# A new written order for the first steps of a two-layer graph network, and looks queued behind the gates

## The chip, the cores and the metric

The kernel runs on one core of a Trainium2 chip. The metric is device microseconds from start to end. The core has five engines with instruction queues of their own: PE (TensorE, matrix products), DVE (VectorE), ACT (ScalarE), POOL (GpSimd) and SP (SyncE, which here only issues transfers). Each executes its queue in order; they wait for each other by semaphores.

## The reference

Sixteen batches of 1024 nodes with 128 features, and one 1024x1024 adjacency matrix of zeros and ones for each. Layer 0 is a gated graph network (four steps, GRU cells), layer 1 a convolution (four steps) with a normalisation over all batches. Both have a norm over the features in front and a residual around.

```python
# layer 0
h = jnp.maximum(_layernorm(x, axis=-1), 0.0)
x = x + gated(h)                # four steps i, for each batch:
#   hw = h @ weight[i];  m = einsum('bjn,bjd->bnd', adj, hw)
#   gx = m @ w_ih[i].T + b_ih[i];  gh = h @ w_hh[i].T + b_hh[i]
#   r = sigmoid(xr + hr); z = sigmoid(xz + hz); n = tanh(xn + r * hn)
#   h = (1 - z) * n + z * h
# layer 1
h = jnp.maximum(_layernorm(x, axis=-1), 0.0)
x = x + conv(h)                 # four steps: adj @ (h @ W[i]) + b[i], relu, norm over (b, n)
```

## The kernel before

`exact_path` does the work; a second path runs only if an entry of the adjacency is found that a 16-bit mantissa can't hold. That finding is the **look** (L568): for each of the eight row blocks of a batch (128 rows, 128x1024 values, 512 KB) DVE takes the maximum of the low 16-bit halves into a column of `low`. All columns are reduced once at the end.

The gated layer runs two batches beside each other, as streams `sa` and `sb` (class `Stream`, L647). Each step of a stream has these parts:

- `split_step` (L688): the features are turned by eight PE transposes into node-major form (at step 0 the normed input `y` has that form already), and split into a high part (ACT) and a low part (DVE), both fp32r, `ghw`.
- `agg_step` (L702): the aggregation, 32 matmuls of 128x512 into the two PSUM banks `pm`, four for each row block: high part to both banks, then low part to both. The weight of the step is folded into the GRU's input matrix, so the aggregation takes the bare features. ACT then copies `pm` to `m`.
- `gate_step` (L713), for each of two halves of 512 nodes: six fp32 products on PE into four PSUM banks `g_r`, `g_hn`, `g_xn`, `g_z`, of which there is one each; sigmoid on ACT (frees `g_r`), two operations on DVE (free `g_hn` and `g_xn`), tanh and sigmoid on ACT (frees `g_z`), three operations on DVE (L738 to L740).

`half_step(one, two)` (L783) puts the gates of one stream and the aggregation of the other after each other. In it `two.ahead()` (L747) prepares the stream's next batch: it loads `x` at step 1, takes its norm at step 2 (`prepare`: statistics on DVE, square root on ACT, scale on DVE, eight ACT blocks `y_in`), and turns it at step 3. `one.look_on()` (L767) starts the transposes of the rows for layer 1 (POOL casts a block to bf16, a transposing DMA follows) and looks at three row blocks a step. From step 1 on only SP and POOL follow the written order; a scheduler lays out PE, DVE and ACT, and `tc.issue_after(ins)` forbids it to put an instruction ahead of `ins` on the same engine. Looks stand behind `self.seen`, the last DVE operation of that stream's own step-0 gates; the norm stands behind the gates' last ACT operation only, so its DVE part stands free.

The first steps (L803 to L847) are written out by hand for all engines. Batch 0 and 1 have no bf16 or fp32r copy in memory, so their rows arrive as raw fp32: four blocks in a `stage` buffer, four in `h` tiles, and POOL or ACT rounds them to fp32r row tiles. The order there: 52 idle transposes on PE; x of batch 0 and 1; rows of batch 0; weights of step 0; norm of x0 whole; aggregation; all eight looks; then the rows of batch 1 into the buffers the looks have left; small vectors, turning of `y`, weights of step 0 (`turn_layer`, L463: seven transposes, a product `w_gT @ w_ihT`, and four DVE copies out of the two PSUM banks `tmp`); norm of x1; gates of batch 0; aggregation and looks of batch 1; weights of steps 1 to 3. Of the `x` tiles there are four, one of them holding `w_g`.

Of the kernel before, what the change touches and what calls it, by code (L numbers as in the profile page):

```python
# [16 lines left out]
P = 128  # L17
# [324 lines left out]
def exact_path(  # L342
# [68 lines left out]
    low = const.tile([P, B * NB], F32, tag="low", name="low")  # L411
# [50 lines left out]

    def turn_layer(prep, w_g, i):  # L463

        pt = tmp(f"pt_whh{i}")
        for g in range(3):
            nc.tensor.transpose(pt[:, g * P : (g + 1) * P], wns["hh", i][:, g, :], ident)
        nc.vector.tensor_copy(w_hhT[:, i, :], pt[:, : 3 * P])
        pt = tmp(f"pt_wih{i}")
        for g in range(3):  # L470
            nc.tensor.transpose(pt[:, g * P : (g + 1) * P], wns["ih", i][:, g, :], ident)

        w_ihT = prep.tile([P, 3 * C], F32, tag="w_ihT", name=f"w_ihT{i}", bufs=1)
        nc.vector.tensor_copy(w_ihT, pt[:, : 3 * P])
        pg = tmp(f"pt_g{i}")
        nc.tensor.transpose(pg[:, :P], w_g[:, i, :], ident)
        w_gT = prep.tile([P, P], F32, tag="w_gT", name=f"w_gT{i}", bufs=1)
        nc.vector.tensor_copy(w_gT, pg[:, :P])
        pw = tmp(f"pt_wm{i}")
        nc.tensor.matmul(pw[:, : 3 * P], w_gT, w_ihT, start=True, stop=True)  # L480
        nc.vector.tensor_copy(w_mT[:, i, :], pw[:, : 3 * P])
# [45 lines left out]
    with ExitStack() as st:  # L527
# [15 lines left out]
        def load_rows_first(b, stage):  # L543

            fs = []
            for j in range(NB):
                if j < 4:
                    f = stage[:, 2 * j : 2 * j + 2, :].rearrange("p a n -> p (a n)")
                else:
                    f = work.tile([P, N], F32, tag="h", name=f"first{b}_{j}", bufs=7)  # L550
                nc.sync.dma_start(f, adj[b][j * P : (j + 1) * P, :])
                fs.append(f)
            return fs
# [14 lines left out]
        def look(b, row, j):  # L568

            lows = row.bitcast(U16).rearrange("p (n t) -> p n t", t=2)[:, :, 0]  # L570
            k = b * NB + j
            nc.vector.tensor_reduce(low[:, k : k + 1], lows, axis=AX.X, op=ALU.max)  # L572
# [7 lines left out]
        def norm(xt, y, name):  # L580

            norm_apply(xt, y, name, norm_stats(xt, name))

        def norm_stats(xt, name):
            stats = small.tile([P, NB, 6], F32, tag="ln_st", name=f"st_{name}")
            mv = small.tile([P, NB, 2], F32, tag="ln_mv", name=f"mv_{name}")
            for k in range(NB):
                nc.vector.bn_stats(stats[:, k, :], xt[:, k, :])
                nc.vector.bn_aggr(mv[:, k, :], stats[:, k, :])
            return mv  # L590

        def norm_apply(xt, y, name, mv, split=None):
            rs = small.tile([P, NB], F32, tag="ln_rs", name=f"rs_{name}")
            nc.scalar.activation(rs, mv[:, :, 1], AF.Sqrt, bias=eps_t)
            nc.vector.reciprocal(rs, rs)
            ms = small.tile([P, NB], F32, tag="ln_ms", name=f"ms_{name}")
            nc.vector.scalar_tensor_tensor(ms, mv[:, :, 0], -1.0, rs, ALU.mult, ALU.mult)
            for k in range(NB):
                nc.scalar.activation(
                    y[:, k * P : (k + 1) * P], xt[:, k, :], AF.Relu, bias=ms[:, k : k + 1], scale=rs[:, k : k + 1]  # L600
                )
                if split and k % BH == BH - 1:
                    split(k // BH)
# [13 lines left out]
        def tail_norm(b, xt, hT):  # L617

            for hf in range(NH):
                pt = tmp(f"pt_x{b}_{hf}")  # L620
                for q in range(BH):
                    k = hf * BH + q
                    nc.tensor.transpose(pt[:, q * P : (q + 1) * P], hT[:, k * P : (k + 1) * P], ident)
                for q in range(BH):
                    k = hf * BH + q
                    nc.vector.scalar_tensor_tensor(
                        xt[:, k, :],
                        pt[:, q * P : (q + 1) * P],
                        maskT[:, b * NB + k : b * NB + k + 1],
                        xt[:, k, :],  # L630
                        ALU.mult,
                        ALU.add,
                    )
            mv = norm_stats(xt, f"mid{b}")
            if b + 1 < B:
                y = work.tile([P, N], F32, tag="h", name=f"y_mid{b}", bufs=7)
            else:
                y = xt.rearrange("p k c -> p (k c)")
            nc.gpsimd.dma_start(xmid_d[b].rearrange("(k p) c -> p k c", p=P), xt)

            def rest():
                norm_apply(xt, y, f"mid{b}", mv)
                nc.gpsimd.dma_start(ymid_d[b], y)

            return rest

        class Stream:  # L647
# [5 lines left out]
            def open(self, xt):  # L653

                self.xt = xt
                self.y = work.tile([P, N], F32, tag=f"y{self.tag}", name=f"y_in{self.b}", bufs=1)
                self.mv = norm_stats(xt, f"in{self.b}")

            def open_split(self):

                self.hw = hw_tiles(self.b, f"ghw{self.b}_0")
                norm_apply(self.xt, self.y, f"in{self.b}", self.mv, self.split_first)

            def open_rows(self, fs, on_scalar):
                self.rows, self.looks = [], NB
                for j, f in enumerate(fs):
                    t = gru_row(self.b, j)
                    if j in on_scalar:
                        nc.scalar.copy(t, f)
                    else:  # L670
                        nc.gpsimd.tensor_copy(t, f)
                    self.rows.append(t)
# [15 lines left out]
            def split_step(self):  # L688
                nm = f"{self.b}_{self.i}"
                self.hw = hw_tiles(self.b, f"ghw{nm}")  # L690
                for g in range(NH):
# [3 lines left out]
                    self.split_first(g)  # L695

            def split_first(self, g):
                hi, lo, y = (t[:, g * HALF : (g + 1) * HALF] for t in (*self.hw, self.y))
                nc.scalar.copy(hi, y)  # L699
                nc.vector.tensor_sub(lo, y, hi.bitcast(F32))  # L700

            def agg_step(self, g):  # L702
                if g == 0:
                    self.pm = [acc(f"m{hf}", f"pm{self.b}_{self.i}_{hf}") for hf in range(NH)]
                aggregate(self.pm, self.hw, self.rows, g)
                if g == NH - 1:
# [6 lines left out]
            def gate_step(self, hf):  # L713
# [20 lines left out]
                nc.vector.tensor_add(r, pxn, r)  # L734
                nc.scalar.activation(r, r, AF.Tanh, bias=b_in(i))  # L735
# [4 lines left out]
                last = nc.vector.tensor_add(ho, ho, r)  # L740
                if i == 0:
                    self.seen = last
# [4 lines left out]
            def ahead(self):  # L747
# [5 lines left out]
                if self.i == 2:  # L753
                    with tc.issue_after(self.last_act.ins):
# [12 lines left out]
            def look_on(self):  # L767
# [10 lines left out]
                with tc.issue_after(self.seen.ins):  # L778
# [4 lines left out]
        def half_step(one, two):  # L783
# [4 lines left out]
            two.gate_step(1)  # L788
            if one.i == 0:
                one.split_step()  # L790
            one.agg_step(0)
            if one.rest:
                with tc.issue_after(two.last_act.ins):
# [3 lines left out]
            one.look_on()  # L797
# [5 lines left out]
        with tc.tile_pool(name="prep", bufs=1) as prep, tc.manual_schedule(engines=every):  # L803
# [3 lines left out]
            for k in range(52):  # L807
                nc.tensor.transpose(pt[:, k % 4 * P : (k % 4 + 1) * P], ident, ident)
            x0, x1 = load_x(0, nc.sync), load_x(1, nc.sync)
            small_in = load_small(prep)  # L810
            stage = keep.tile([P, NB, N], BF16, tag="adjT", name="stage", bufs=1).bitcast(F32)
            rows0 = load_rows_first(0, stage)
            h0 = work.tile([P, N], F32, tag="h", name="h_in0", bufs=7)
            load_layer(0)
            w_g = flat("w_g")[:, :L, :]
            nc.sync.dma_start(w_g, g_weight.rearrange("l c d -> c l d"))

            sa.open(x0)
            sa.open_split()
            sb.open(x1)  # L820
            sa.open_rows(rows0, (4, 5, 6, 7))
            sa.agg_step(0)
            for j, f in enumerate(rows0):
                look(0, f, j)
            rows1 = load_rows_first(1, stage)
            for i in range(1, L):
                load_layer(i)
            h1 = work.tile([P, N], F32, tag="h", name="h_in1", bufs=7)
            sa.agg_step(1)
            turn_small(*small_in)  # L830
            turn(sa.y, "in0", h0)
            turn_layer(prep, w_g, 0)
            sa.hT = h0
            sb.open_split()
            turn(sb.y, "in1", h1)
            sb.hT = h1
            sb.open_rows(rows1, ())
            nc.gpsimd.dma_start(w_c, c_w.rearrange("l c d -> c l d"))
            sa.gate_step(0)
            sa.gate_step(1)  # L840
            sb.agg_step(0)
            sb.agg_step(1)
            for j, f in enumerate(rows1):
                look(1, f, j)
            for i in range(1, L):
                turn_layer(prep, w_g, i)
            sa.ahead()  # L847
        with tc.manual_schedule(engines={mybir.EngineType.Pool, mybir.EngineType.SP}):
            for s in range(1, B // 2 * L):
# [260 lines left out]
```

## Time and profile before

| what | value |
|---|---|
| median of 3 runs | 1871.44 us (1869.63 to 1871.64) |
| profiled execution | 1870.41 us |
| its span, first to last instruction | 1868.6 us |
| PE busy | 1827.9 us, 98% |
| DVE / ACT / POOL busy | 65% / 56% / 15% |
| granted PE clock | 0.991 of full, mean |

The gated layer takes the first 1250 us or so, the convolution the rest. A matmul's time in the profile is its latency; how densely PE works shows in the distance between starts. A row of the timeline has its start, its time, the engine and line, what is written from what, how many instructions it merges, and in brackets the idle time before it and what ended that.

### The profile page before, as it was taken

The numbers are of one execution on the slowest core, as the hardware profiler recorded it, in microseconds if no ns is written. First come the engines' busy times: TensorE is split into PE (matmuls) and PEld (weight loads), VectorE is DVE, ScalarE is ACT, GpSimd is POOL, SyncE is SP. The second block draws the span as 40 slices with busy tenths as digits, with TensorE's granted clock in tenths as the row PEclk, the third lists the DMA queues.
The fourth block names the chain that finished last, engine by engine and source line by source line (L and its number), as shares of the span: only waits on it lengthen the run. The fifth ranks groups of instructions, "written<-read, shape, count | busy, mean of one in ns | idle before, by whom it ended". The sixth has DMA issues, their size and how long they took to land.

```text
span 1868.6 us, 21940 instructions
## 1 busy us (share of the span) xinstructions
PE 1827.9 (98%) x7328; PEld 1257.9 (67%) x7328; DVE 1215.2 (65%) x2242; ACT 1041.8 (56%) x1569; POOL 287.8 (15%) x369
## 2 busy tenths in 40 slices
PE   7999999999999999999999999999999999999995
PEld 5666656565656666666656665667778888888884
DVE  5746864775684595586476577576666666666664
ACT  4353553554454455455356453357777768768764
POOL 3121230221042032023023113000000000000021
PEclk8999999999999999999999999999999999999998
DMA  7487476485376567557548546339876676666768
GB/s 260 118 231 259 156 204 191 149 239 179 124 225 198 186 166 228 192 162 204 217 139 224 169 149 145 128 126 334 301 245 228 212 250 214 237 235 216 251 211 260
DMA packets 267824, 381.21 MB, mean 204 GB/s; under 512 B 149716, under 2 KB 171896, under 8 KB 263864
## 3 DMA queue, kind: packets, MB, share of 16 engines
q1 hardware_dynamic: 250032, 246.21, 43.7%
q0 software_dynamic: 17456, 133.45, 20.3%
q8 instruction: 59, 0.97, 0.2%
q14 instruction: 61, 0.50, 0.1%
q10 hardware_dynamic: 216, 0.08, 0.0%
HBM read 287.39 MB, written 117.44 MB: 217 GB/s over the span
## 4 chain that ended last, share of the span: by engine, by line
PE 42%; issue 5%; DVE 3%; DMA 3%; POOL 1%; ACT 1%; SPq 0%; DVEq 0%; POOLq 0%; ACTq 0%
PE pc_m L518 12%; PE pc_g_z L518 6%; PE pc_g_r L518 6%; PE pm L518 4%; PE hw_c L493 4%; PE g_z L722 2%; PE g_r L722 2%; DMA adjT<-half 2%; DVE low L572 1%; PE g_xn L722 1%; PE pt_o L1054 1%; PE g_hn L722 1%; PE pw_g_hn L935 1%; PE pw_g_xn L935 1%; PE pc_g_r L503 1%
## 5 line engine op out<-in xcount | busy, mean ns | idle before, releaser
L518 PE MATMUL pm<-row,ghw 128*128 128x512 f32 x2048 | 506.7, 404 | 2.1 <-ACT ghw L699 2.1
L518 PEld LDWEIGHTS pm<-row,ghw 128*128 128x128 f32 x2048 | 385.0, 189 | 107.4 <-issue 31.9
L518 PE MATMUL pc_m<-wide,chw 128*128 128x512 f32 x1024 | 246.1, 396 | 0.0
L518 PEld LDWEIGHTS pc_m<-wide,chw 128*128 128x128 f32 x1024 | 190.6, 188 | 42.2 <-issue 4.3
L735 ACT ACTIVATE r<-r,vecs 128x512 f32<-128x512 f32 x128 | 92.3, 721 | 213.3 <-DVE r L734 213.2
L518 PE MATMUL pc_g_r<-wide,chw 128*128 128x512 f32 x464 | 187.2, 404 | 0.3 <-ACT chw L495 0.3
L518 PE MATMUL pc_g_z<-wide,chw 128*128 128x512 f32 x464 | 181.3, 391 | 0.0
L577 POOL CAST half<-row 128x1024 bf16<-128x1024 f32 x128 | 141.5, 1122 | 247.0 <-DMA adjT<-half 166.4
L880 DVE CAST wide<-packed 128x1024 fp32r<-128x1024 bf16 x160 | 110.3, 693 | 74.6 <-PE pc_m L518 56.3
L880 DVE CAST wide<-block 128x1024 fp32r<-128x1024 bf16 x160 | 110.3, 692 | 73.3 <-PE pc_g_z L518 35.1
L736 ACT ACTIVATE z<-g_z,brz 128x512 f32<-128x512 f32 x128 | 87.3, 682 | 121.2 <-PE g_z L722 121.2
L496 DVE TENSOR_TENSOR ghw<-hw_g,ghw 128x512 fp32r<-128x512 f32 x96 | 61.7, 683 | 118.7 <-ACT ghw L495 118.7
L722 PE MATMUL g_xn<-m,w_mT 128*128 128x512 f32 x256 | 131.9, 597 | 4.9 <-DVE r L734 4.9
L878 ACT CAST wide<-block 128x1024 fp32r<-128x1024 bf16 x96 | 100.6, 1048 | 60.9 <-PE pc_m L518 34.4
L878 ACT CAST wide<-packed 128x1024 fp32r<-128x1024 bf16 x96 | 100.7, 1049 | 56.5 <-PE pc_g_z L518 27.4
L722 PE MATMUL g_r<-m,w_mT 128*128 128x512 f32 x256 | 131.6, 596 | 0.0
L572 DVE TENSOR_REDUCE low<-row 128x1 f32<-128x1024 uint16 x112 | 130.8, 1201 | 0.0
L722 PE MATMUL g_z<-m,w_mT 128*128 128x512 f32 x256 | 130.8, 593 | 0.0
L732 ACT ACTIVATE r<-g_r,brz 128x512 f32<-128x512 f32 x128 | 87.7, 685 | 61.0 <-PE g_r L722 59.8
L738 DVE TENSOR_TENSOR h<-h,r 128x512 f32<-128x512 f32 x96 | 68.9, 718 | 78.7 <-ACT r L735 78.7
L733 DVE SCALAR_TENSOR_TENSOR r<-g_hn,vecs,r 128x512 f32<-128x512 f32 x128 | 95.0, 742 | 35.8 <-PE g_hn L722 18.6
L710 ACT COPY m<-pm 128x512 f32<-128x512 f32 x128 | 68.0, 582 | 87.5 <-PE pm L518 87.5
(142 smaller groups left out, 2774.0 us busy)
## 6 DMA issues: line engine op xcount, KB each, us to landing
packed<-adjT_d SPq DMA_DIRECT2D x256, 256.0 KB, 5.7
block<-adjT_d SPq DMA_DIRECT2D x256, 256.0 KB, 5.3
raw<-in_adj_dram POOLq DMA_DIRECT2D x112, 512.0 KB, 11.7
row<-raw SPq DMA_DIRECT2D x112, 512.0 KB, 6.2
adjT_d<-adjT POOLq DMA_DIRECT2D x16, 2048.0 KB, 7.2
xmid_d<-x POOLq DMA_DIRECT2D x16, 512.0 KB, 4.2
y<-ymid_d POOLq DMA_DIRECT2D x16, 512.0 KB, 5.4
xo<-xmid_d POOLq DMA_DIRECT2D x32, 256.0 KB, 6.1
```

What stands on the lines that cost most here:

```text
L493: nc.tensor.matmul(pt[:, q * P : (q + 1) * P], src, w, start=True, stop=True)
L518: nc.tensor.matmul(pm[hf], hw[s][:, j * P : (j + 1) * P], rows[j][:, hf * HALF : (hf + 1) * HALF], start=(j == 0 and s == 0), stop=(j == N ...
L572: nc.vector.tensor_reduce(low[:, k : k + 1], lows, axis=AX.X, op=ALU.max)
L577: nc.gpsimd.tensor_copy(t, row.bitcast(F32))
L722: nc.tensor.matmul(po, wT[:, i, g * C : (g + 1) * C], rhs, start=start, stop=stop)
L732: nc.scalar.activation(r, pr, AF.Sigmoid, bias=brz[:, 3 * i : 3 * i + 1])
L733: nc.vector.scalar_tensor_tensor(r, phn, b_hn(i), r, ALU.add, ALU.mult)
L735: nc.scalar.activation(r, r, AF.Tanh, bias=b_in(i))
L736: self.last_act = nc.scalar.activation(z, pz, AF.Sigmoid, bias=brz[:, 3 * i + 1 : 3 * i + 2])
L738: nc.vector.tensor_sub(ho, hin, r)
L878: nc.scalar.copy(r, t)
L880: nc.vector.tensor_copy(r, t)
```

## The change

It does five things. The norm of x0 is taken in two halves, x0 arrives in two halves through two queues (SP and ACT). The turning of `y`, the small vectors and the weights of step 0 stand between the row blocks 3 and 6 of the first aggregation. The rows of batch 1 are loaded into unused tiles first (the first four blocks as eight halves), ahead of the looks; a look at a half row has a column of its own, so `low` grows by two batches of columns and is cleared. The norm of x1 stands beside the first gates, and the weights of steps 1 to 3 each between two half steps. And in the rest of the gated layer the looks are put behind the last DVE operation of the other stream's gates just before them, the norm behind the last ACT and the last DVE operation of the gates.

```diff
     def turn_layer(prep, w_g, i):
...
         nc.vector.tensor_copy(w_gT, pg[:, :P])
+        turned[i] = w_gT, w_ihT
+
+    def join_layer(i):
+        w_gT, w_ihT = turned[i]
         pw = tmp(f"pt_wm{i}")
         nc.tensor.matmul(pw[:, : 3 * P], w_gT, w_ihT, start=True, stop=True)
         nc.vector.tensor_copy(w_mT[:, i, :], pw[:, : 3 * P])
...
+        def behind(*inss):
+
+            es = ExitStack()
+            for ins in () if written[0] else inss:
+                es.enter_context(tc.issue_after(ins.ins))
+            return es
...
+                if between:
+                    between()
                 nc.scalar.activation(r, r, AF.Tanh, bias=b_in(i))
...
                 if self.i == 2:
-                    with tc.issue_after(self.last_act.ins):
+                    with behind(self.last_act, self.last_dve):
                         self.prepare(self.b + 2, self.next_x)
...
-            def look_on(self):
+            def look_on(self, two):
...
-                with tc.issue_after(self.seen.ins):
+                with behind(two.last_dve):
                     while self.looks < min(3 * self.i, NB):
...
-        def half_step(one, two):
+        def half_step(one, two, gated=None, halfway=None):
...
             two.gate_step(1)
+            if gated:
+                gated()
...
             one.agg_step(0)
+            if halfway:
+                halfway()
...
-            for k in range(52):
+            for k in range(50):
...
-            x0, x1 = load_x(0, nc.sync), load_x(1, nc.sync)
+            x0 = flat("x0")
+            for k0, eng in ((0, nc.sync), (BH, nc.scalar)):
+                x0_d = x[0].rearrange("(k p) c -> p k c", p=P)[:, k0 : k0 + BH, :]
+                eng.dma_start(x0[:, k0 : k0 + BH, :], x0_d)
...
+            first_rows(0, range(4), quarters)
             load_layer(0)
...
+            nc.sync.dma_start(w_g[:, 0, :], w_d[:, 0, :])
+            first_rows(0, range(4, NB), late)
+            x1 = load_x(1, nc.sync)
...
+            first_rows(1, range(4), halves)
...
+            sa.sums(range(4))
+            norm_root(sa.norm, 0, BH)
+            sa.sums(range(4, 5))
+            norm_scale(sa.norm, 0, BH)
+            sa.sums(range(5, NB))
+            sa.normed(range(2))
+            norm_root(sa.norm, BH, NB)
+            norm_scale(sa.norm, BH, NB)
+            sa.normed(range(2, 4))
+            sa.split_high(0)
+            for j in range(4):
+                sa.rows[j] = first_round(0, j, raw0[j], nc.gpsimd)
+            first_look(0, 0, raw0[0])
+            sa.split_low(0)
+            sa.agg_rows(range(4))
+            sa.normed(range(4, NB))
+            sa.split_high(1)
+            first_look(0, 1, raw0[1])
+            sa.split_low(1)
+            for j, eng in ((4, nc.scalar), (5, nc.gpsimd)):
+                sa.rows[j] = first_round(0, j, raw0[j], eng)
+
+            turn_small(*small_in)
+            turn(sa.y, "in0", h0)
+            sa.hT = h0
+            first_look(0, 2, raw0[2])
+            turn_layer(prep, w_g, 0)
+            first_look(0, 3, raw0[3])
+            first_rows(1, range(4, NB), quarters)
+            sa.agg_rows(range(4, 6))
+            join_layer(0)
+            for j, eng in ((6, nc.scalar), (7, nc.gpsimd)):
+                sa.rows[j] = first_round(0, j, raw0[j], eng)
+            sa.agg_rows(range(6, NB))
+
+            sb.sums(range(NB))
+            norm_root(sb.norm, 0, NB)
+            norm_scale(sb.norm, 0, NB)
+            for j in range(NB):
+                sb.rows[j] = first_round(1, j, raw1[j], nc.gpsimd)
+
+            def beside(hf):
+                sb.normed(range(hf * BH, (hf + 1) * BH))
+                first_look(0, 4 + hf, raw0[4 + hf])
+
+            for hf in range(NH):
+                sa.gate_step(hf, lambda: beside(hf))
+                sb.split_high(hf)
+                sb.split_low(hf)
+            for j in (6, 7):
+                first_look(0, j, raw0[j])
+            for j in range(4):
+                first_look(1, j, raw1[j])
...
+            sb.agg_rows(range(4))
             turn(sb.y, "in1", h1)
             sb.hT = h1
+            sb.agg_rows(range(4, NB))
             sa.ahead()
+
+            def looks():
+                for j in range(4, NB):
+                    first_look(1, j, raw1[j])
+
+            half_step(sa, sb, looks, lambda: turn_layer(prep, w_g, 1))
+            join_layer(1)
+            half_step(sb, sa, None, lambda: turn_layer(prep, w_g, 2))
+            join_layer(2)
+            turn_layer(prep, w_g, 3)
+            join_layer(3)
...
-            for s in range(1, B // 2 * L):
+            written[0] = False
+            for s in range(2, B // 2 * L):
                 half_step(sa, sb)
                 half_step(sb, sa)
```

`first_rows` loads row blocks, `first_round` rounds them on ACT or POOL, `first_look` looks at each part; `norm_sums`, `norm_root`, `norm_scale` and `norm_blocks` are the four parts of the norm, and `sums`, `normed`, `split_high` and `split_low` call them and the two parts of the split for a stream.

As built, the scheduler's order of the rest of the gated layer changes with it. Before, all eight looks of a batch stand in one row on DVE, partly between the operations of the gates. After, they stand in threes behind the gates; in the half step in which a stream reaches step 2, DVE has the statistics of the next batch's norm and three looks behind the gates, then the norm's scale, then the low parts of the split, and ACT has the eight `y_in` blocks ahead of the high parts (in the next half step between the two high parts). PE has four matmuls of the aggregation pulled between the two halves of the gates there, and nine in the next half step.

## The prediction

> **What bounds the kernel now.** First the page: the busy times and the forty slices.
>
> ```profile
> PE 1827.9 (98%) x7328; PEld 1257.9 (67%) x7328; DVE 1215.2 (65%) x2242; ACT 1041.8 (56%) x1569; POOL 287.8 (15%) x369
> ...
> PE   7999999999999999999999999999999999999995
> ```
>
> PE sets the end. Only time in which PE waits, or runs at half clock, can be won. I took dense distances between PE starts from the timeline (0.227 us for an aggregation matmul, 0.43 for a gate's, 0.109 for a turn) and summed what exceeds them: 47.7 us in the whole span. Of it 17.8 lie between the first aggregation (11.88) and the end of the second aggregation of batch 1 (98.95), 10.4 in the looks' stages between 200 and 1200, 9 at the last normalisation, which the change leaves alone.
>
> The first steps, in stretches of 10 us (after each engine's busy time comes the granted clock):
>
> ```profile
> 10.00:20.00 10.00, 8.12 (x28) 6.27 (x29) 6.46 (x21) 7.87 (x13) 2.91 (x3) 0.83 0.91 330
> 20.00:30.00 10.00, 4.71 (x21) 3.43 (x20) 7.54 (x11) 2.44 (x5) 4.95 (x5) 0.68 0.98 347
> 30.00:40.00 10.00, 7.30 (x18) 3.15 (x17) 2.60 (x7) 6.68 (x13) 5.10 (x6) 0.67 0.92 270
> 40.00:50.00 10.00, 10.00 (x25) 4.68 (x24) 7.64 (x24) 2.81 (x6) 0.00 (x0) 0.96 0.00 0
> ```
>
> Then the timeline of DVE and PE there:
>
> ```profile
> 22.25 4.59 DVE L572 TENSOR_REDUCE low<-first 128x1 f32<-128x1024 uint16 x4
> 26.76 0.18 DVE L448 COPY vecs<-pt_v 128x36 f32<-128x36 f32 x1
> ...
> 11.88 9.39 PE L518 MATMUL pm<-row,ghw 128*128 128x512 f32 x32 [2.09 <-ACT ghw L699]
> ...
> 27.00 1.97 PE L613 MATMUL pt_in<-ident,y_in 128*128 128x128 f32 x8 [5.29 <-DVE vecs L448]
> ...
> 33.79 1.63 PE L613 MATMUL pt_in<-ident,y_in 128*128 128x128 f32 x4 [1.48 <-ACT y_in L599]
> ...
> 37.41 1.92 PE L722 MATMUL g_r<-h_in,w_hhT 128*128 128x512 f32 x2
> ```
>
> A 0.18 us copy stands behind eight looks and holds PE for 5.3 us; the clock falls, and the first gates start at 37.41 although their aggregation ended at 21.27.
>
> Then a look stage, timeline at 238 us:
>
> ```profile
> 238.30 1.20 DVE L572 TENSOR_REDUCE low<-row 128x1 f32<-128x1024 uint16 x1
> 239.42 0.68 DVE L734 TENSOR_TENSOR r<-g_xn,r 128x512 f32<-128x512 f32 x1
> ...
> 240.15 1.13 PE L722 MATMUL g_xn<-m,w_mT 128*128 128x512 f32 x2 [0.60 <-DVE r L734]
> ```
>
> Looks between the gates' DVE operations free the one bank `g_xn` late. Such half steps take up to 1.4 us more than an undisturbed one; per pair of batches 1.8, 1.1, 2.2, 1.3, 1.5, 1.2 and 1.3 us, together 10.4.
>
> **The first steps, worked out.** x0's first half should land at 4.4, an estimate: the whole let DVE start at 4.99, less about half of the 1.29 us that 512 KB take here. Four blocks of statistics at 0.395: 6.0. Root 0.30, one more block, reciprocal 0.20, scale 0.54: 7.15. Two `y_in` blocks 0.85: 8.05. The second root waits for statistics until 8.4 and ends at 8.7, two blocks 9.5, high part 0.62: PE starts at 10.15, not 11.88. Row 0 is looked at before the low part is made (9.3 to 11.15), which costs PE 0.6. Rows 0 to 3 end at 14.4. x1 now loads behind all rows of batch 0, so these rows land no later (17.2 for the last, at the 1.29 us a block of before).
>
> From 14.4 to 17.1 PE does small vectors, turning and seven transposes, 1.84 us of work; each waits for a `tmp` bank that DVE (0.18 to 0.56 a copy, one look of 1.14 between) or ACT (0.59) empties: 0.9 lost. Rows 4 and 5: 18.95. Product: 19.6. Rows 6 and 7: 21.4. The first gates start at 21.4, 16.0 earlier, at full clock, and end at 31.7. Beside them: statistics of x1 20.2 to 23.4, table load 1.28, sigmoid free at 25.75; the second half's `g_r` needs it at 26.6, so no wait. Batch 1's blocks land until 28.8 (9.5 MB at the same pace) and POOL has rounded them by 30; block 4 is wanted at 36.2. The norm's second low part comes at 36.8 and costs 0.15. Batch 1's aggregation ends at 40.0 (before: 56.7).
>
> Gates of batch 1: 40.9 to 51.2. DVE owes ten looks from 36.8 (two whole, eight halves at about 0.6, estimated from 1.14 a whole) until 43.9; `g_hn` is wanted at 47.7, so hidden.
>
> Then the new wait. PE's order is four row blocks, the transposes of step 1's weights, four blocks. DVE ends the gates at 53.9 and has four looks (4 x 1.145) ahead of the copy `w_hhT`: 58.5, copied at 59.1. `pt_g` is the third user of two banks and has stood since 55.5: 3.6 lost, and behind it the rest of the aggregation. Half clock after it: before, 2.1 us of idle at 9.8 was followed by one cold stretch of 3.4 us in which 16 matmuls took 0.427 each; I put 1.3 of the possible 1.7. The joins and steps 2 and 3 lose 1.5 more, their copies being only 0.5 apart from the products.
>
> Sum of losses 0.6 + 0.9 + 0.15 + 3.6 + 1.3 + 1.5 = 8.05, so (11.88 + 17.8) - (10.15 + 8.05) = **11.5 us won**. Bounds: x0's half could land with the whole (0.6 less) and each new gap could bring its own cold stretch (2.8 less), or neither the 1.3 nor half of the small waits come (2.5 more): 8 to 14.
>
> POOL is let go later: `x` of batch 3 waits for the tile of `w_g`, whose last turn moves from 71 to about 88, and behind it in POOL's queue stand the raw copies and casts, behind these SP's transposes. They end by 165; batch 2's rows are wanted at 173. Hidden by 10 us; without that cover each late us costs one.
>
> Costed at nothing: the clearing of `low` (DVE waits for x0 until 4.4), two idle transposes fewer, the half x0 issued by ACT ahead of its table load (0.65 more; the load ended at 4.47 and the root is wanted at 6.0; without that cover 0.1), 16 more columns in the last reduction, and SP's loads of the later weights behind tiles that the looks free at 44 (about 48; wanted at 54.8, each us beyond would lengthen the new wait).
>
> The Trainium skill, "TensorE: Matmul & The Clock Gate", Part 4, says that transposes don't count as PE work for the clock. This trace shows otherwise: its idle transposes go from 0.213 to 0.109 us apart at 6.8 and PE starts warm. By the page the transposes put between the rows would let the clock fall once more, 1.7 us at its half rate; by the row nothing.
>
> **The looks, worked out.** Gone: 10.4. New: in the half step in which a stream reaches step 2, everything is queued behind the gates. Let T be the gates' end on PE. DVE ends the gates at T+h; statistics 2.2, three looks 3.45, reciprocal and scale 0.45; ACT then has eight `y_in` blocks 3.18, the two high parts 1.05, a table load 1.30, and only then the sigmoid 0.69 that frees `g_r`: T+h+12.4. PE wants it at T + 7.27 (aggregation) + 0.87 + 5.16 (half the gates) + 0.91 (four pulled matmuls) = T+14.2. Wait: h - 1.8. In the next half step nine matmuls are pulled and one high part comes first: h - 2.6. The rows for the prices:
>
> ```profile
> 265.93 3.19 ACT L599 ACTIVATE y_in<-x,ms_in,rs_in 128x128 f32<-128x128 f32 x8 [0.47 <-DVE ms_in L597]
> ...
> 271.05 1.28 ACT L732 ACT_TABLE_LOAD   x1
> ...
> 277.11 1.41 DVE L739 TENSOR_TENSOR h<-h,z 128x512 f32<-128x512 f32 x1
> ```
>
> Undisturbed, h is 2.4. Beside POOL's casts it was 2.3 to 5.0 (the third line: 1.41, not 0.69), and casts fall in both half steps. I take 3.2 for both, nearer to the half steps without a second table load: 1.4 + 0.6 = 2.0 a pair, in the six pairs that have both norm and looks: 12.0. Net **1.8 lost**. Bounds: h = 2.4 gives 0.6 x 6 = 3.6, net 6.8 won; h = 4.9 and 4.2 give (3.1 + 1.6) x 6 = 28, net 18 lost.
>
> Total 11.5 - 1.8 = 9.7 from the profiled 1870.4: 1860.7. The median of the runs lies 1.0 above that execution: **1862**. Own range 1856 to 1867.
>
> **Rivals.** (1) *Both gains come*: POOL's casts miss the gates, h is 2.4: 11.5 + 6.8 = 18 won, 1853. For it: in three of seven pairs h was 2.3 to 2.4 in the second of these half steps. Against: POOL's casts fill 4 to 6 us around the first. (2) *The norm held up by the looks becomes the bound, slower*: one mechanism, the chain statistics, looks, scale, `y_in`, sigmoid, in twelve half steps. At 4.7 a pair 18 are lost against 11.5 won: 1878. It decides from 3.65 a pair ((11.5 + 10.4) / 6). For it: POOL casts in every such pair. Against: it needs nearly the highest h of the trace in each. (3) *The first steps give back more*: the stall before step 1's weights grows as DVE is later than I have it, each gap goes cold, and 11.5 shrinks to 3: 1870. For it: DVE has no slack between 20 and 59. Against: PE's waits up to 51 have 0.8 to 4 us of room.
>
> **How the numbers follow.** Forecast 0.53, (1) 0.17, (2) 0.12, (3) 0.18. No change means within 0.2% (3.7 us), 1867.7 to 1875.2; a measurement of this kernel tells no less. Faster: 0.51 + 0.17 + 0.03 = 0.71; same: 0.02 + 0.03 + 0.14 = 0.19; slower 0.10. The range reaches from (1) to short of (2): 1853 to 1874.
>
> **What would show it.** Right: first aggregation at about 10.2; first gates at about 21.4 and end of batch 1's first aggregation near 40; PE waiting 3 to 4 us at `pt_g` behind `w_hhT` near 55; no PE wait for L734's bank `g_xn` among looks; in pairs 1 to 6 a PE wait of 1 to 2 us at `g_r` for ACT's sigmoid once a pair, none in the last pair. Wrong: gates starting after 26, a PE wait at the aggregation for rows or for `ghw` in the first steps, waits at `g_r` over 3 us in each pair, or batch 2's rows late.

## The result, and the profile after

The changed kernel takes 1866.06 us (median of 12 runs, 1864.58 to 1869.47) against 1871.64 for the kernel before beside it (12 runs, 1869.32 to 1872.88). The medians lie 5.6 us apart; the ratio is 0.9973, 95% interval 0.9964 to 0.9982: between 3.4 and 6.7 us won. Predicted were 1862 and a gain of 9.7; 1866.06 lies inside the forecast's own range and at its upper end.

The profiled execution has a span of 1863.3 us (before 1868.6). The page's rows that answer to those of before:

```profile
PE 1825.8 (98%) x7326; PEld 1255.0 (67%) x7326; DVE 1226.6 (66%) x2249; ACT 1032.4 (55%) x1562; POOL 290.3 (16%) x375
...
PE   9999999999999999999999999999999999999995
```

The 7 in the first slice has become a 9. The first steps in the same stretches of 10 us (PE, PEld, DVE, ACT, POOL busy, then the granted clock):

```profile
10.00:20.00 10.00, 8.88 (x35) 6.19 (x36) 6.02 (x11) 5.50 (x10) 3.96 (x4) 0.83 1.03 360
20.00:30.00 10.00, 10.00 (x32) 5.72 (x31) 6.54 (x24) 4.88 (x9) 6.69 (x10) 1.00 1.05 391
30.00:40.00 10.00, 9.74 (x37) 5.84 (x35) 9.21 (x12) 6.79 (x13) 4.28 (x5) 1.00 0.34 96
40.00:50.00 10.00, 9.72 (x35) 6.04 (x36) 9.78 (x15) 2.84 (x7) 0.00 (x0) 1.00 0.35 98
...
60.00:70.00 10.00, 7.42 (x28) 5.69 (x29) 3.83 (x7) 1.71 (x4) 0.00 (x0) 0.83 0.00 0
```

From 20 to 40 PE is now busy 10.00 and 9.74 of each 10 us, where it had been busy 4.71 and 7.30. The lost time now sits in the first and the last of these rows. The timelines of PE and DVE show both places:

```profile
10.41 0.70 PE L525 MATMUL pm<-row,ghw 128*128 128x512 f32 x2 [1.47 <-ACT ghw L733]
11.42 5.06 PE L525 MATMUL pm<-row,ghw 128*128 128x512 f32 x14 [0.31 <-DVE ghw L737]
...
24.00 1.02 PE L762 MATMUL g_r<-h_in,w_hhT 128*128 128x512 f32 x2
...
40.28 3.48 PE L525 MATMUL pm<-row,ghw 128*128 128x512 f32 x14 [0.47 <-DVE ghw L737]
...
62.37 0.33 PE L479 MATMUL pt_g<-ident,w_g 128*128 128x128 f32 x1 [3.10 <-DVE w_hhT L471]
62.45 5.50 PE L525 MATMUL pm<-row,ghw 128*128 128x512 f32 x16
...
57.26 4.59 DVE L589 TENSOR_REDUCE low<-stage 128x1 f32<-128x1024 uint16 x4
61.77 0.55 DVE L471 COPY w_hhT<-pt_whh 128x384 f32<-128x384 f32 x1
```

The first gates start at 24.00 (before 37.41, predicted 21.4). The wait at `pt_g` behind four looks is there as predicted (3.10), and the 16 matmuls behind it take 5.34 us, from the first one's start to the start of what follows, in place of 3.63. What was not predicted is that the 14 matmuls at 11.42 take 5.06 us. The same two places by granted clock (the same columns as above):

```profile
10.00:13.40 3.40, 2.67 (x8) 1.89 (x9) 3.19 (x4) 2.44 (x6) 1.87 (x2) 0.81 0.97 321
13.40:16.80 3.40, 3.40 (x11) 2.36 (x10) 0.10 (x1) 1.04 (x1) 1.04 (x1) 0.68 1.02 414
62.00:65.40 3.40, 3.03 (x10) 2.41 (x11) 1.03 (x3) 0.00 (x0) 0.00 (x0) 0.70 0.00 0
65.40:68.80 3.40, 3.40 (x15) 2.59 (x13) 0.16 (x1) 1.03 (x2) 0.00 (x0) 0.80 0.00 0
```

In the later pairs of batches no wait at `g_xn` is left. In its place, PE waits once or twice a pair for the sigmoid on ACT. One such half step in the timelines of DVE, ACT and PE:

```profile
388.29 0.69 DVE L782 TENSOR_TENSOR h<-h,r 128x512 f32<-128x512 f32 x1
...
390.93 1.19 DVE L589 TENSOR_REDUCE low<-row 128x1 f32<-128x1024 uint16 x1
...
392.13 2.31 DVE L589 TENSOR_REDUCE low<-row 128x1 f32<-128x1024 uint16 x2
...
394.58 0.17 DVE L618 SCALAR_TENSOR_TENSOR ms_in<-mv_in,rs_in 128x8 f32<-128x8 f32 x1
...
394.78 3.19 ACT L622 ACTIVATE y_in<-x,ms_in,rs_in 128x128 f32<-128x128 f32 x8 [1.28 <-DVE ms_in L618]
...
400.23 0.69 ACT L772 ACTIVATE r<-g_r,brz 128x512 f32<-128x512 f32 x1
...
400.97 1.13 PE L762 MATMUL g_r<-h,w_hhT 128*128 128x512 f32 x2 [1.02 <-ACT r L772]
```

This is read down: the gates' last operation on DVE, three looks, the norm's scale only behind them, `y_in` on ACT, the sigmoid, and PE, which had stood for a microsecond.

For sums over many such places I add up, from the trace's PE starts, what each distance has beyond the dense one (0.227 us for an aggregation matmul, 0.4295 for a gate's). Between 200 and 1200 us that gives 10.8 for the kernel before and 11.8 for the changed one.

### The profile page after: what moved, and what is told of

The parts are those of the page before. It is cut to its first block, busy times and chain, and to the rows that moved or that the text cites. A ratio compares the mean times of both kernels' runs of the same rounds, so it can differ in the third digit from the quotient of the medians.

```text
span 1863.3 us, 21952 instructions
## 1 busy us (share of the span) xinstructions
PE 1825.8 (98%) x7326; PEld 1255.0 (67%) x7326; DVE 1226.6 (66%) x2249; ACT 1032.4 (55%) x1562; POOL 290.3 (16%) x375
## 5 line engine op out<-in xcount | busy, mean ns | idle before, releaser
L525 PE MATMUL pm<-row,ghw 128*128 128x512 f32 x2048 | 520.1, 408 | 2.4 <-ACT ghw L733 1.5
L1023 DVE BATCH_NORM_STATS2 stats<-feat 128x6 f32<-128x512 f32 x128 | 84.2, 685 | 48.8 <-ACT feat L1022 47.5
```

The source lines that it names most:

```text
L525: nc.tensor.matmul(pm[hf], hw[s][:, j * P : (j + 1) * P], rows[j][:, hf * HALF : (hf + 1) * HALF], start=(j == 0 and s == 0), stop=(j == N ...
L1023: nc.vector.bn_stats(stats[:, b * NH + hf, :], dst)
```

## The experiments

Times are medians, those of e9, e10 and e11 single executions. The experiments come in groups, each with its own runs of the kernel before (1870.75, 1869.84, 1870.12), so across groups I compare the ratios to before: a difference of 0.001 is 1.9 us.

**The two parts, each alone.** e1 has the new first steps and the old rules for looks and norm:

```diff
+                if i == 0:
+                    self.seen = self.last_dve
...
-                    with behind(self.last_act, self.last_dve):
+                    with behind(self.last_act):
...
-                with behind(two.last_dve):
+                with behind(self.seen):
```

> The new first steps with the old rules for looks and norm behind them (looks behind the stream's own step-0 gates, norm behind the last ACT operation alone). Theory: the two parts of the change add up. From equal places in the two traces the first steps won 7.2 us (the half steps stand 6.8 to 7.4 earlier from 110 us to 280 us), and the looks' part lost about 1.1. So this kernel should stand 7 us below the kernel before, about 1864.5, 1 to 1.5 us below the changed kernel; the looks should cost PE the old 10.4 between 200 and 1200 us, in waits at g_xn. Rival: the first steps won less, and the looks' part brought part of the gain: then this kernel ends at 1868 or above.

Measured: 1861.0, ratio 0.9948 (0.9935 to 0.9962). The first steps alone win 9.75 us (7.1 to 12.2; 7 expected). The kernel stands 4.7 below the changed one, more than the 1 to 1.5 expected. PE's loss between 200 and 1200 us is 8.1 (10.4 expected), all in the old form.

e2 is the kernel before with the new rules alone:

```diff
-                if i == 0:
-                    self.seen = last
+                self.last_dve = last
...
-                    with tc.issue_after(self.last_act.ins):
+                    with tc.issue_after(self.last_act.ins), tc.issue_after(self.last_dve.ins):
...
-                with tc.issue_after(self.seen.ins):
+                with tc.issue_after(two.last_dve.ins):
```

> The kernel before with the new rules for looks and norm alone. Theory: PE's waits at g_xn among looks (10.4 us) go, and waits at g_r behind ACT's sigmoid come, 1.8 us a pair in six pairs (11 us), so the time stays within 2 us of the kernel before, about 1872.5. Rival 1: the looks' part is worth several us and the first steps hid it: 1866 to 1868. Rival 2: it costs more where POOL is not let go late: 1876.

Measured: 1875.41, ratio 1.0020 (1.0011 to 1.0029). The new rules alone lose 4.7 us (2.1 to 5.4). The waits are those expected, 12.3 us between 200 and 1200 us, none at `g_xn`. The two parts add up: 9.75 - 4.7 = 5.1, where the changed kernel wins 5.6. So the looks' part brought none of the gain. The time is nearer to rival 2's 1876 than to 1872.5, but not for its reason: the new rules cost PE no more here (12.3) than in the new first steps with POOL let go late (11.8). What the old rules cost is the open side.

**How far one profile can be trusted.** Two kernels were profiled a second time, unchanged.

> The kernel before, a second profiled execution. Theory: what PE loses to looks between 200 and 1200 us (10.8 in the first profile) comes from the order on DVE and repeats within 1 us, and the clock's fall in the first 17 us does not repeat exactly, so that the first gates start up to 2 us from 37.4. Rival: the 10.8 was one draw; the old rules in new first steps lost 8.1 and 8.2, so this execution shows 8 to 9 as well.

Measured: 1868.7, and 8.7 us lost between 200 and 1200 us where the first profile has 10.8. Its rival held. With the old rules four executions (two of the kernel before, e1, e7) now show 10.8, 8.7, 8.1 and 8.3, a mean of 9.0; with the new rules six (the changed kernel twice, e2, e3, e4, e11) show 11.5 to 13.3, a mean of 12.3. The first gates started at 38.7, not 37.4.

> The changed kernel, a second profiled execution. Theory: the half clock between 10 and 17 us in its first profile is a draw (of six executions with the same gap of 1.4 to 1.5 us before the first aggregation two were cold, of two without the gap none), so it may be missing here, rows 0 to 3 then end at 14.4, while the wait of 3.1 us at pt_g and the waits at g_r (11.8 lost between 200 and 1200 us) repeat within 1.5 us. Rival: the first profile's cold stretch belongs to the code: rows 0 to 3 end at 16.4 again.

Measured: 1865.89. Rows 0 to 3 end at 15.97, cold again, so the rival's outcome came, and the expectation had its premise wrong: the gap ahead of the first aggregation is not the same in all those executions. The row of PE's timeline with the first aggregation shows it, in e1, e4 and e10, which have the same code up to there:

```profile
10.37 4.12 PE L525 MATMUL pm<-row,ghw 128*128 128x512 f32 x16 [0.41 <-ACT ghw L733]
```

```profile
10.30 4.16 PE L525 MATMUL pm<-row,ghw 128*128 128x512 f32 x16 [1.48 <-ACT ghw L733]
```

```profile
10.35 5.69 PE L525 MATMUL pm<-row,ghw 128*128 128x512 f32 x16 [1.92 <-ACT ghw L733]
```

The 50 idle transposes start at 1.36 in all, but they quicken from 0.213 to 0.109 us apart anywhere between 4.2 and 7.4 us, and so end at different times.

**The gap.** e3 has 64 idle transposes in place of 50, e11 has 36.

```diff
-            for k in range(50):
+            for k in range(64):
```

> The changed kernel with 64 idle transposes in place of 50, so that they end at about 10.4 us, when the first aggregation starts, not at 8.9. Theory: the 1.47 us without PE work before the first aggregation lets the clock fall (granted 0.81 and 0.68 between 10 and 16.8 us), which costs rows 0 to 3 about 1.9 us; without the gap the clock stays at 1.00 there, rows 0 to 3 end at about 14.5 in place of 16.4 and the time falls by 1.5 to 1.9 us. Rival 1: transposes don't count for the clock, or its fall has to do with what PE did before: no change. Rival 2: the aggregation is quicker but waits for rows (block 4 is rounded at 15.3, block 5 later): less than 1 us won.

> The changed kernel with 36 idle transposes in place of 50: PE has no work for about 3 us before the first aggregation. Theory: whether the clock falls depends on how much of a span of some 3.4 us is without work; with a gap of 3 us it falls always, as in four of five executions behind the 3.1 us wait at pt_g, and rows 0 to 3 end at 16 to 16.4. Rival: the idle transposes have no part in the clock's state: rows 0 to 3 end at 14.4, as in four of six executions with the gap of 1.5 us.

Measured: e3 1864.23, ratio 0.9972 (0.9959 to 0.9984), by its ratio the same as the changed kernel. e11 1865.86. In the traces, rows 0 to 3 end at 14.51 in e3 and at 16.05 in e11:

```profile
10.42 4.16 PE L525 MATMUL pm<-row,ghw 128*128 128x512 f32 x16
```

```profile
10.37 5.74 PE L525 MATMUL pm<-row,ghw 128*128 128x512 f32 x16 [3.33 <-ACT ghw L733]
```

Over eleven executions with these first steps: no cold stretch with no gap or one of 0.32 to 0.81 us (e3, e6, e12, e1, e7, e8), one cold and one warm at 1.47 and 1.48 (the changed kernel, e4), cold at 1.72, 1.92 and 3.33 (e5, e10, e11). So the cold stretch goes with the gap, but 1.47 and 1.48 stand on both sides. The same traces settle why. In each of them the granted clock changes only at moments that lie whole multiples of 3.41 us apart (in the changed kernel at 5.32, 12.14, 15.55, 63.34 and 66.75); where these moments lie differs from execution to execution. What the falls go with is PE's time without work between two such moments, all its waits there together:

| execution | stretch | PE without work in it | clock in the next stretch |
|---|---|---|---|
| changed kernel | 8.73 to 12.14 | 1.78 (1.47 and 0.31) | 0.50 |
| e4 | 8.47 to 11.88 | 1.48 | 1.00 |
| e5 | 8.75 to 12.16 | 1.71 | 0.50 |
| changed kernel | 59.93 to 63.34 | 2.44 | 0.50 |
| e3 | 56.28 to 59.69 | 1.71 | 1.00 |
| e3 | 59.69 to 63.10 | 1.39 | 1.00 |

In the first 100 us of all fourteen traces, each of the sixteen stretches at full clock with 1.78 us or more without work was followed by half clock, and none with 1.48 or less; 1.71, half of a stretch, came out both ways. So the theory recorded for e11 held, and whether a gap of 1.5 to 3 us costs anything depends also on where it falls.

That closing the gap shortens the whole kernel was not shown. e3's trace has the first gates of batch 0's step 1 at 66.85, 2.9 us earlier than the changed kernel's, but there the clock did not fall behind `pt_g` either, by the chance of where those moments lay. The two ratios agree, and their intervals of 0.1% to either side are as wide as the 1.9 us in question. e3's six runs stand in two groups, four at 1862.3 to 1864.5 with a mean clock of 0.995 or 0.996 and two at 1868.6 with 0.993; where the clock fell in the slower ones is not known.

**The wait at `pt_g`.** e4 moves the four looks behind the copy of the product:

```diff
-            half_step(sa, sb, looks, lambda: turn_layer(prep, w_g, 1))
+            half_step(sa, sb, None, lambda: turn_layer(prep, w_g, 1))
             join_layer(1)
+            looks()
```

> The changed kernel with the four last looks of batch 1 moved from before the copies of step 1's weights to behind the product's copy. Theory: the wait of 3.1 us at pt_g goes, and with it the half clock in the 16 matmuls behind it (1.7 us): the time falls by 4.3 to 5 us, to about 1861.5, and the first gates of batch 0's step 1 start at about 65, not 69.75. Rival: the wait comes back in another place, since DVE's four looks (4.6 us) now stand ahead of the low parts and of the gates' first DVE operation: PE waits at g_hn or g_xn of the second half, 1 to 3 us, and less than 3 us are won.

Measured: 1860.31, ratio 0.9944 (0.9930 to 0.9957): 5.4 us below the changed kernel. PE's timeline of e4, then three rows of DVE's:

```profile
58.37 0.33 PE L479 MATMUL pt_g<-ident,w_g 128*128 128x128 f32 x1 [0.33 <-DVE w_hhT L471]
58.46 3.91 PE L525 MATMUL pm<-row,ghw 128*128 128x512 f32 x16
...
64.15 1.02 PE L762 MATMUL g_r<-h,w_hhT 128*128 128x512 f32 x2
...
63.04 0.56 DVE L488 COPY w_mT<-pt_wm 128x384 f32<-128x384 f32 x1 [4.01 <-PE pt_wm L487]
63.52 4.59 DVE L589 TENSOR_REDUCE low<-stage 128x1 f32<-128x1024 uint16 x4
68.02 1.28 DVE L503 TENSOR_TENSOR ghw<-hw_g,ghw 128x512 fp32r<-128x512 f32 x2
```

The wait is 0.33, the 16 matmuls behind it run at full clock, and the gates of step 1 start at 64.15, against 68.56 in e1, whose first 50 us went like these. No wait comes back. The looks end at 68.1; the low parts behind them are wanted only after the gates, at 74.05, and the gates' first DVE operation empties `g_hn` at 69.96, where PE wants it at 71.02. DVE's 4.0 us without work before the product's copy stay unused.

**The chain behind `g_r`.** e5 puts the looks behind the norm's scale, so that the norm no longer stands behind them:

```diff
-                with behind(two.last_dve):
+                with behind(two.last_dve, *([two.scaled] if two.i == 2 and two.b + 2 < B else [])):
```

(`two.scaled` is the norm's last DVE operation.)

> The changed kernel, but in the half step that takes the next batch's norm the looks stand behind the norm's scale on DVE, not only behind the gates. Theory: what PE waits for at g_r is the chain gates' end on DVE, statistics, three looks, scale, y_in, table load, sigmoid (in the changed kernel the wait is within 0.4 us of the gates' lag h less 1.8 in the first such half step and less 2.6 in the second). With 3.45 us of looks out of the chain the sigmoid is ready 3 to 5 us before PE wants it: the waits at g_r (10.2 us in twelve half steps) go, PE loses at most 2 us between 200 and 1200 us, and the time falls by 9 to 10 us against the changed kernel, to about 1856. Rival 1: ACT's queue (y_in, copies of pm, table load) is late by itself: the waits stay over half. Rival 2: the looks behind the norm hold up the low parts of the split or the next gates: PE waits at the aggregation for ghw or at g_xn, and less than 4 us are won.

Measured: 1857.42, ratio 0.9931 (0.9918 to 0.9945): 7.9 us below the changed kernel. PE loses 4.2 us between 200 and 1200 us, where at most 2 were expected; none of it is a wait that PE's list of waits shows. The same half step as above, in e5's timelines of DVE, ACT and PE:

```profile
390.29 0.17 DVE L618 SCALAR_TENSOR_TENSOR ms_in<-mv_in,rs_in 128x8 f32<-128x8 f32 x1
390.37 3.46 DVE L589 TENSOR_REDUCE low<-row 128x1 f32<-128x1024 uint16 x3
...
390.49 3.19 ACT L622 ACTIVATE y_in<-x,ms_in,rs_in 128x128 f32<-128x128 f32 x8 [0.47 <-DVE ms_in L618]
...
396.90 0.69 ACT L773 ACTIVATE r<-g_r,brz 128x512 f32<-128x512 f32 x1
...
397.72 1.05 PE L763 MATMUL g_r<-h,w_hhT 128*128 128x512 f32 x2
```

From the scale to the sigmoid's start it is 6.6 us here and 5.65 in the changed kernel: ACT has both copies of `pm` in this chain now, so the sigmoid is not as early as the 3 to 5 us I expected. It is in time nevertheless: PE has no wait before `g_r`. The scheduler also laid PE out anew (two matmuls of the aggregation stand before this `g_r`, not four), so the edit moved more than the looks.

e8 leaves the looks at batches 2 to 15 out altogether.

> The changed kernel without the looks at batches 2 to 15 (they are left out; only the finding for batches 0 and 1 is made). Theory: the looks in the chain are all that PE loses in the gated layer's later part: without them the sigmoid at g_r is never late, PE loses under 1 us between 200 and 1200 us, and the time is that of the kernel with the norm first, about 1855 to 1856. Rival: the waits at g_r come from POOL's casts beside DVE or from ACT's queue: they stay at 1 us or more in each pair and the time stays above 1862.

Measured: 1857.41, ratio 0.9934 (0.9920 to 0.9947), 3.9 us lost between 200 and 1200 us: the same as e5 in time and within 0.3 us in PE's loss. So the order is all that the looks cost; behind the norm they are free. The loss is not under 1 us, as was expected: what is left is there without any look.

**Together.** e6 has the edits of e3, e4 and e5; e7 has e1's rules and e4's edit, with 50 idle transposes; e12 is e6 with two more looks moved behind the low parts of batch 1's first split:

```diff
                 sb.normed(range(hf * BH, (hf + 1) * BH))
-                first_look(0, 4 + hf, raw0[4 + hf])
...
-            for j in (6, 7):
+            for j in range(4, NB):
                 first_look(0, j, raw0[j])
```

> The changed kernel with three edits: looks behind the norm's scale, the four last looks of batch 1 behind the product's copy, 64 idle transposes. Theory: they lie in different places and add up: 9 to 10 from the first, about 5 from the second, 0 to 2 from the third: 1850 to 1852. Rival: the earlier start puts POOL's casts and transfers where they hold up the gates: 1855 or above.

> The changed kernel with the old rules for looks and norm and with the four last looks of batch 1 behind the product's copy. Theory: the first steps alone stood at 1861, the moved looks win 4.5 to 5 us as they did under the new rules: about 1856. It says what the old rules are worth beside the norm put first: the old rules lose 8 to 10 us between 200 and 1200 us, so it should end 4 to 8 us above the kernel with all three edits. Rival: the old rules lose nothing more once the first steps are shorter: within 2 us of it.

> The kernel with all three edits, and the looks at blocks 4 and 5 of batch 0 moved from between the first gates' DVE operations to behind the low parts of batch 1's split. Theory: PE loses 1.2 to 2.4 us in batch 1's first aggregation because each half's low part stands behind one look more on DVE (0.66 us of it in front of the second half's low part in every execution); with the looks behind them these waits go, and the ten looks still end near 47, before the gates of batch 1 want DVE: 1 to 1.5 us won against the kernel with all three edits, about 1851. Rival: the h operations wait for tanh on ACT anyway, behind y_in, so the low part comes no sooner: no change.

Measured: e6 1852.39, ratio 0.9905 (0.9890 to 0.9920), 17.5 us below the kernel before and by the ratios 12.7 below the changed one: the fastest of all, and nearly the sum of its parts (7.9 + 5.4 + 0.2). e7 1856.03 beside it, 3.6 above e6, a little less than the 4 to 8 expected; e6's 14 more idle transposes may be part of the difference. e12 1852.81, ratio 0.9901 (0.9885 to 0.9918): no change, so the rival held. Without the look between, DVE stands 0.79 us for the tanh, and its `h` operations beside POOL's casts take 1.34 and 1.41; the first low part starts at 33.35, against 32.93 in e6.

## Why the prediction was right in sign and too high in size

**The first steps** were put at 11.5 us (8 to 14). e1 gives 9.75, inside the bounds. The trace gives 8.2, measured at the start of batch 0's gates of step 2 (118.27, 118.39 and 119.31 in three executions with the old first steps, on average 110.5 in five with the new ones). Term by term, in the changed kernel's first profile and in e1:

| term of the sum | predicted | changed | e1 |
|---|---|---|---|
| first aggregation starts | 10.15 | 10.41 | 10.37 |
| lost in rows 0 to 3 | 0.6 | 2.36 | 0.42 |
| small vectors, turning, weights, rows 4 to 7 | 0.9 | 1.5 | 1.5 |
| lost in batch 1's first aggregation | 0.15 | 1.2 | 2.0 |
| wait at `pt_g` | 3.6 | 3.3 | 3.3 |
| half clock behind it | 1.3 | 1.7 | 1.7 |
| joins, steps 2 and 3 | 1.5 | 1.9 | 1.9 |

With these losses the sum gives about 7.3 won in the changed kernel's trace and 8.5 in e1's. The large new wait and its half clock together were sized to 0.1 (the prediction counts 16 matmuls in the cold stretch of the kernel before; its trace shows seven distances of 0.427). The starts and the order were right as well: without a cold stretch rows 0 to 3 end at 14.4, exactly where the prediction has them. Two terms failed, and two small ones were 0.4 and 0.6 short. "PE starts warm" was argued from where the idle transposes quicken; the gap behind them was left out of the sum, although the kernel before shows a cold stretch behind a gap of 2.1; only the lower bound allowed for it. And the first aggregation of batch 1 was charged only its second low part, 0.15. There PE waits 0.5 for the second half's low part and, from execution to execution, nothing to 1.3 (e8) for the first half's, whose DVE operations take up to 1.41 us, not 0.69, beside POOL's casts. e12 shows that taking the looks away from there does not bring it sooner. A PE wait for `ghw` in the first steps was one of the prediction's own signs of being wrong, and it is this one.

**The looks** were put at 1.8 lost, with 12.0 new and 10.4 gone (which makes 1.6). The new side was right, mechanism and size: with h read from the changed kernel's six pairs (3.0 to 4.0 in the first half step, 2.65 to 3.3 in the second), the waits are h - 2.1 and h - 2.5, where h - 1.8 and h - 2.6 stood, and they add up to 10.2. e5 and e8 show that the looks in this chain make the waits: behind the norm, or left out, PE does not wait at `g_r`. The side that failed is "Gone: 10.4": it was one execution's value, and the highest of four; the mean is 9.0. The means differ by 12.3 - 9.0 = 3.3, the medians of e2 and of e1 beside the changed kernel by 4.7; the 1.4 between the two figures is not explained.

So 11.5 - 1.8 became about 9.75 - 4.7. POOL was let go at 92.6, later than the 88 foreseen, and no wait for batch 2's rows appears, as predicted. Rival (1) needed h = 2.4 and falls. Rival (2) had the mechanism right; its price of 4.7 a pair did not come (1.7). Rival (3) was partly right: the first steps did give back more, about 2 to 3 us.

On the clock the Trainium skill ("TensorE: Matmul & The Clock Gate", the table "Why this matters for your kernels") asks for no gaps in PE's work over about 3 us. Here gaps of 1.47, 1.72 and 1.92 us were followed by half clock, and one of 1.48 was not, so the measurement sets a tighter rule: by the table above, some 1.7 us without work between two of the clock's possible changes. Its Part 4, weighed in the prediction, has transposes not count as PE's work; e3 and e6 speak against it, since there nothing but transposes fills the gap, and the clock stays at full.

## What to carry to other kernels

When low-priority work is moved from between latency-critical operations to behind them, ask what else starts there: the looks cost nothing once they stood behind the norm (e5 against e8), and 8 us while the norm stood behind them, although the rule that put them there had removed every wait it was meant for. Do not put such work in front of a copy on which PE's order depends: behind the copies, the same four looks cost nothing (e4). And a term taken from a single profile has the scatter of a single profile: a second one of the same kernel differed by 2 us in the very sum that was to be won.

## What was not expected of the hardware

The same 50 idle transposes, started at 1.36 us, reach full speed between 4.2 and 7.4 us after the span's start, from execution to execution, so that the gap they leave before the first real work varies from 0.4 to 1.9 us by itself. Behind the wait of 3.1 us at `pt_g` the clock fell in the changed kernel (both profiles), e1, e5, e8 and e11, but not in e3, whose wait was as long: there one of the moments at which the clock can change, 59.69, cut the wait into 1.71 and 1.39 us.
